# Differential attention with a feed-forward interleaved: moving when a block's inputs and the feed-forward pieces are issued

## The chip, the cores and the metric

The kernel runs on one core of a Trainium2 chip. The core has a matrix engine (TensorE, "PE" in the profile), a vector engine (VectorE, "DVE"), an engine for activation functions (ScalarE, "ACT"), a general engine (GpSimd, "POOL") and DMA queues ("SP" and others). They run side by side and wait for each other by semaphores. The metric is the time of one execution on the device in microseconds (us); lower is better.

## The reference

Four blocks are applied to `x`, of 2 batches by 1024 tokens by 256 channels, each added to its input: softmax attention, a small feed-forward, a second attention and the small feed-forward again; then differential attention, a gated feed-forward with 4-bit weights, a recurrent layer that learns while it runs, and the gated feed-forward again. What is changed lies in the differential attention and the first gated feed-forward:

```python
energy = jnp.einsum('bqhad,bkhad->bahqk', qd, kd)      # a: two halves of each head
energy = jnp.where(causal, NEG, energy)
scores = jax.nn.softmax(energy / np.sqrt(D), axis=-1)
diff = scores[:, 0] - lam * scores[:, 1]
diff = jnp.where(causal, NEG, diff)
diff = jax.nn.softmax(diff, axis=-1)
att = jnp.einsum('bhqv,bvhd->bqhd', diff, v)
att = att * rsqrt(mean(att * att) + EPS) * rms_w * (1 - LAM_INIT)
x = x + att @ Wo
x = x + (gelu(xn @ Wg.T) * (xn @ Wu.T)) @ Wd.T         # xn: layernorm of x
```

There are 16 heads with 4 key heads, of width 2 x 16 for queries and keys and 16 for values. The hidden width of the feed-forward is 2048. Everything is float32.

## The kernel before, in words

`build` runs the stages one after the other: attention, attention, feed-forward, then `attn_d_ffn1` (the differential attention and the gated feed-forward of its tiles) and `ttt_ffn1` (the recurrent layer and the last feed-forward). Only `attn_d_ffn1` is touched.

**Blocks, pairs, rounds.** Queries are cut into 8 blocks `i` of 128 tokens. A block has 8 pairs of heads in batch 0 and then 8 in batch 1, so 16 pairs; 128 pairs in all. The main loop runs over rounds `n`. Round `n` issues the scores of pair `n` (L1209), the masked row maxima (`highest`, VectorE, L1220) and the exponentials (ScalarE, L1230), and the later steps of the pairs before it: `ratio` (L1236), `difference` (L1252), `turn` (transposes on TensorE, L1267, then an exponential on ScalarE, L1274) and, for every second pair, `weigh` (L1287). Blocks 4 to 7 have more than 512 keys and are "large": their scores come in two parts. So rounds 0 to 63 are small and 64 to 127 large, and a few more rounds follow in which only later steps are left.

**Filling pieces.** Between these steps each round issues pieces of other work, kept in the dictionary `at` by round and added with `add(n, step)`. They are
- the inputs of a block (`attn_d_inputs`: layernorm statistics, normalized rows, the transpose `xT`), and then for each batch five pieces from `attn_d_block`: `queries` (a projection of 512 columns, then a rotation on VectorE and GpSimd), `keys` (the same with 192 columns, and a copy of the values by ScalarE, L1150), `turn_queries(0)`, `turn_queries(1)` (transposes, then a ScalarE copy into `qT`, L1160) and `turn_keys` (transposes, then two VectorE multiplications into `kT`, L1167);
- the output of a block (`attn_d_out`: `squares`, `root`, `normalize`, `project`);
- the feed-forward of a block's tokens (`ffn1_parts`: `stats`, `rows`, `turn`, 8 `gate` pieces, `gelu`, 8 `up` pieces, 8 `down` pieces).

A large round splits its list of filling pieces in three parts, in the order of the `add` calls; a small round splits it in two.

**Order.** `in_order` keeps TensorE, VectorE, ScalarE and GpSimd in the order in which the program issues instructions. An engine that waits holds up everything behind it.

**The one bank.** Every filling piece with a matmul takes its PSUM tile from `bank` (L1095). In small rounds two banks take turns; in large rounds there is one. A piece then can't start its matmuls before the engine that reads the piece before has emptied that bank. The accumulator of the `down` pieces holds it from the first of the eight to the last.

**Places.** Counted from the first round of block `i`, its inputs stood at -9, -8, -6; then batch 0 at -4, -4, -2, -2, -2 and batch 1 five times at -1. For block 0 all are issued ahead of round 0. The output and feed-forward of block `i` are counted from the first round of block `i+1`, a round later for blocks 0 to 2. Those of block 7 belong to the next stage, except for its output.

Of the kernel before, what the change touches and what calls it, by code (L numbers as in the profile page):

```python
# [23 lines left out]
NB = T // P  # L24
# [20 lines left out]
class Net:  # L45
# [899 lines left out]
    def attn_d_ffn1(self, w, wo, cos, sin, nlam, rms_w, deq):  # L945
# [7 lines left out]
        with ExitStack() as ctx:  # L953
# [35 lines left out]
            def add(n, *steps):  # L989
                at.setdefault(max(n, -1), []).extend(steps)  # L990

            for i in range(NB):
                n = 16 * i
                tile_ = type("tile", (), {})()
                blocks = [
                    self.attn_d_block(pools, tile_, b, i, kT[b], v[b]) for b in range(B)
                ]
                for m, step in zip(
                    (-9, -8, -6, -4, -4, -2, -2, -2, -1, -1, -1, -1, -1),
                    (*self.attn_d_inputs(ps, work, tile_, i), *blocks[0][0], *blocks[1][0]),  # L1000
                ):
                    add(n + m if i else -1, step)
                for _, units in blocks:
                    pairs.extend(units)

                n += 16
                squares, root, normalize, project = self.attn_d_out(ps, work, tile_, wo, i)
                if i == NB - 1:

                    for m, step in enumerate((squares, root, normalize, project)):  # L1010
                        add(n + 2 + m, step)
                    continue
                stats, rows, turn, gate, gelu, up, down = self.ffn1_parts(ps, work, i, deq)
                n += 1 if i < 3 else 0
                for m, step in (
                    (2, squares), (3, root), (4, normalize), (5, project), (5, stats), (6, rows),
                    (7, turn), *((8 + k // 2, gate[k]) for k in range(8)), (12, gelu),
                    *((13 + k // 2, up[k]) for k in range(8)),
                    *((17 + k // 2, down[k]) for k in range(8)),
                ):  # L1020
                    add(n + m, step)
            nothing = type("nothing", (), {"large": False})()

# [19 lines left out]
            for n in range(max(max(at), max(weighings)) + 1):  # L1043
# [8 lines left out]
                k = (len(fill) + 2) // 3, (2 * len(fill) + 2) // 3, (len(fill) + 1) // 2  # L1052
# [1042 lines left out]
```

## Time and profile before

| what | value |
|---|---|
| median of 3 runs | 3026.88 us (3020.59 to 3034.16) |
| the profiled execution's own time | 3026.56 us |
| its span, first to last instruction | 3024.8 us |
| TensorE busy | 2592.0 us, 86% of the span |
| VectorE busy | 1949.4 us, 64% |
| ScalarE busy | 1324.3 us, 44% |
| GpSimd busy | 1037.1 us, 34% |
| rounds 0 to 127 of the changed stage | about 1067.7 to 2161.8 us of the span |

A round is read off the trace by the first score matmul (L1209) of each pair. The table below names the rounds that matter later by their place in a block; the clock is the granted share of TensorE's clock, a mean.

| rounds | from, to (us) | TensorE busy | VectorE busy | clock |
|---|---|---|---|---|
| block 6, round 14 (2 `up`, 3 input pieces of batch 0) | 1950.7, 1963.6 | 10.75 | 9.20 | 1.00 |
| block 6, round 15 (2 `up`, 5 input pieces of batch 1) | 1963.6, 1989.6 | 15.06 | 12.27 | 0.82 |
| block 7, round 14 (2 `up`) | 2142.0, 2151.8 | 9.80 | 8.38 | 1.00 |
| block 7, round 15 (2 `up`) | 2151.8, 2161.8 | 8.55 | 9.67 | 1.00 |

Busy time of TensorE counts a matmul from its start to a modelled end, so it shows where the engine has something to do and not how well it does it.

### The profile page before, as it was taken

Reading aid. Unit: us, or ns where it says so; the run is one execution under the profiler, and the core shown is the slowest. Engines: PE = TensorE matmul, PEld = TensorE weight load, DVE = VectorE, ACT = ScalarE, POOL = GpSimd, SP = SyncE. Lnnn points to the kernel's source line nnn. Section 1 sums busy time; section 2 is a strip of 40 time slices with the busy share of each in tenths; the row PEclk is TensorE's granted clock in tenths of the full one; section 3 lists DMA queues with packets and bytes.
Section 4 is the critical chain, followed back from the end, with each engine's and each line's share of the span. In section 5 each row is a group of like instructions: output and inputs, shape, how many; then the busy total and the mean of one; then the engine's idle time right before and its main releaser. Section 6 shows DMA issues by size and latency. Waiting matters only on the chain.

```text
span 3024.8 us, 66879 instructions
## 1 busy us (share of the span) xinstructions
PE 2592.0 (86%) x26384; PEld 1613.2 (53%) x26384; DVE 1949.4 (64%) x6736; ACT 1324.3 (44%) x2672; POOL 1037.1 (34%) x1672
## 2 busy tenths in 40 slices
PE   6999997999988777889888778888877888888888
PEld 2334344434434444666555555555555766677777
DVE  5777665866755456757677868768646656565552
ACT  2686850454453256566565555646521212212110
POOL 3345322212115466556565646556500000000000
PEclk8999997999999856889899888988987889998999
DMA  3000000000001100000000000000001100101100
GB/s 116 1 1 1 1 1 1 1 1 1 1 15 43 28 1 1 1 1 1 1 1 1 1 1 1 1 1 1 20 15 24 24 21 19 23 14 33 24 9 15
DMA packets 61979, 35.39 MB, mean 12 GB/s; under 512 B 43216, under 2 KB 58080, under 8 KB 61664
## 3 DMA queue, kind: packets, MB, share of 16 engines
q1 hardware_dynamic: 59472, 29.49, 3.8%
q8 instruction: 208, 3.41, 0.5%
q10 hardware_dynamic: 2192, 1.61, 0.2%
q14 instruction: 107, 0.88, 0.1%
HBM read 22.68 MB, written 8.39 MB: 10 GB/s over the span
## 4 chain that ended last, share of the span: by engine, by line
PE 38%; DVE 13%; ACT 7%; issue 5%; POOL 3%; DMA 0%; POOLq 0%; ACTq 0%; DVEq 0%
PE ph L1420 6%; PE po L1929 5%; PE pg L1916 4%; PE pu L1916 4%; ACT p L1230 4%; PE e L1209 3%; DVE p L1220 3%; PE dT L1267 3%; PE po L1439 2%; DVE p L1256 2%; PE py L1287 2%; PE pq L232 1%; POOL p L1243 1%; PE pq L1599 1%; PE kh L1599 1%
## 5 line engine op out<-in xcount | busy, mean ns | idle before, releaser
L1220 DVE CUSTOM_DVE_ANT_0 p<-e,mask 128x512 f32<-128x512 f32 (+3 forms) x768 | 381.1, 552 | 67.8 <-PE e L1209 67.3
L1230 ACT ACTIVATE p<-p,nm 128x128 f32<-128x128 f32 (+7 forms) x512 | 389.7, 764 | 51.3 <-DVE nm L1220 39.6
L1274 ACT ACTIVATE pT<-dT 128x128 f32<-128x128 f32 (+7 forms) x256 | 165.6, 647 | 285.5 <-PE dT L1267 284.2
L1209 PE MATMUL e<-kT,qT 32*128 32x512 f32 (+3 forms) x1536 | 243.9, 607 | 44.9 <-DVE nm L1220 43.3
L196 POOL TENSOR_SCALAR ln_mv<-ln_mv 128x2 f32<-128x2 f32 x56 | 18.1, 324 | 728.4 <-DVE ln_mv L194 718.4
L1243 POOL TENSOR_SCALAR p<-p,ra,neg_lam 128x128 f32<-128x128 f32 (+7 forms) x256 | 215.9, 843 | 145.8 <-DVE ra L1239 120.2
L1267 PE MATMUL dT<-ident,p 128*128 128x128 f32 x1152 | 194.2, 300 | 56.0 <-ACT pT L1274 29.9
L845 ACT ACTIVATE pr<-s 128x512 f32<-128x512 f32 (+3 forms) x384 | 157.3, 496 | 162.9 <-PE s L840 154.2
L1256 DVE CUSTOM_DVE_ANT_0 p<-p,rs 128x128 f32<-128x128 f32 (+7 forms) x256 | 206.4, 832 | 32.0 <-POOL p L1247 31.9
L1267 PEld LDWEIGHTS dT<-ident,p 128*128 128x128 f32 x1152 | 147.8, 153 | 133.8 <-issue 48.2
L1260 POOL TENSOR_SCALAR p<-p,md 128x128 f32<-128x128 f32 (+7 forms) x256 | 207.0, 809 | 25.4
L550 ACT ACTIVATE pr<-s 128x1024 f32<-128x1024 f32 (+1 forms) x192 | 145.4, 813 | 131.1 <-PE s L544 82.8
L1929 PE MATMUL po<-down,inter 128*128 128x256 f32 x576 | 162.0, 444 | 6.7 <-issue 5.6
L1916 PE MATMUL pg<-xT,gate 128*128 128x256 f32 x576 | 152.8, 412 | 8.5 <-ACT xT L225 5.5
L805 PE MATMUL s<-kT,qT 32*128 32x512 f32 (+3 forms) x768 | 155.0, 518 | 4.3 <-DVE q_pad L813 2.5
L555 ACT ACTIVATE pr<-pr 128x1024 f32<-128x1024 f32 (+1 forms) x192 | 152.1, 852 | 0.0
L1420 PE MATMUL ph<-xT,up 128*128 128x256 f32 x448 | 126.2, 433 | 27.5 <-DVE inter L1428 20.5
L813 DVE CUSTOM_DVE_ANT_0 masked<-s,mask 128x128 f32<-128x128 f32 (+3 forms) x256 | 110.6, 487 | 59.2 <-PE s L805 59.0
L1209 PEld LDWEIGHTS e<-kT,qT 32*128 32x128 f32 x1536 | 91.9, 213 | 103.4 <-DVE nm L1220 74.1
L1259 POOL TENSOR_SCALAR md<-md 128x1 f32<-128x1 f32 x256 | 90.9, 355 | 161.4 <-DVE md L1256 149.6
L1929 PEld LDWEIGHTS po<-down,inter 128*128 128x128 f32 x576 | 126.8, 225 | 31.2 <-issue 7.0
L558 POOL TENSOR_SCALAR_AFFINE_SELECT pr<-pr 128x256 f32<-128x256 f32 x128 | 90.4, 724 | 153.2 <-ACT pr L555 56.2
(313 smaller groups left out, 5418.5 us busy)
## 6 DMA issues: line engine op xcount, KB each, us to landing
uk_d<-uk SPq DMA_DIRECT2D x128, 32.0 KB, 1.9
r<-uk_d SPq DMA_DIRECT2D x8, 512.0 KB, 3.9
x<-in_L_attn_a_X SPq DMA_DIRECT2D x4, 512.0 KB, 6.0
qh_d<-qh SPq DMA_DIRECT2D x8, 256.0 KB, 2.8
o<-qh_d SPq DMA_DIRECT2D x128, 16.0 KB, 1.8
out<-x SPq DMA_DIRECT2D x4, 512.0 KB, 3.1
w<-in_L_ffn_W2T SPq DMA_DIRECT2D x1, 1024.0 KB, 8.1
pk<-in_L_ffn_gate_packed SPq DMA_DIRECT2D x8, 128.0 KB, 2.5
```

The lines of the kernel that those rows point to most:

```text
L845: nc.scalar.activation(pr[:, g, off:512], tiles[g][:, 0:m], AF.Exp, scale=0.25)
L1209: nc.tensor.matmul(own.tiles[h][:, a, 0 : hi - lo], made["q"][r : r + 32, a, t, :], kT[r : r + 32, a, lo:hi], start=True, stop=True,)
L1220: nc.vector.tensor_tensor_reduce(own.p[h][a][:, lo:hi], own.tiles[h][:, a, 0 : hi - lo], neg_row[:, T - nk + lo : T - nk + hi], -1.0, 3e38 ...
L1230: nc.scalar.activation(own.p[h][a], own.p[h][a], AF.Exp, bias=own.nm[:, h, a : a + 1], scale=-1.0, accum_out=own.sm[:, h, a : a + 1],)
L1243: nc.gpsimd.tensor_scalar(p1, p1, own.ra[:, h : h + 1], nlam[:, head : head + 1], ALU.mult, ALU.mult)
L1256: nc.vector.tensor_tensor_reduce(p0, p0, p1, own.rs[:, h, 0:1], -3e38, ALU.add, ALU.max, md)
L1260: nc.gpsimd.tensor_scalar(p0, p0, md, 1.0, ALU.add, ALU.mult)
L1267: nc.tensor.transpose(dT[:, kb, :], own.p[h][0][:, kb * P : (kb + 1) * P], self.ident)
L1274: nc.scalar.activation(pT[:, 0 : qb + 1, :], dT[:, 0 : qb + 1, :], AF.Exp)
L1420: nc.tensor.matmul(ph[:, j, :], w[:, kc, m * P : (m + 1) * P], f.xT[:, kc, :], start=(kc == 0), stop=(kc == 1),)
L1916: nc.tensor.matmul(ph[:, j, :], m_[:, kc, m * P : (m + 1) * P], f.xT[:, kc, :], start=(kc == 0), stop=(kc == 1),)
L1929: nc.tensor.matmul(f.po[:, b], inter[m // 2][:, m % 2, b * P : (b + 1) * P], wd[:, m % 2, (m // 2) * C : (m // 2 + 1) * C], start=(m == 0) ...
```

## The change

It alters two lists of rounds, and adds two lines for one block; the steps and their work stay.

- Inputs: after the three common ones, batch 0's pieces stand at -5, -4, -3, -2, -1, one to a round. Batch 1's `queries` and `keys` move behind the start of the block, to 0 and 1, and its three transposing pieces to 7, the last round of batch 0's pairs. Block 0 follows the same rule: what would be ahead of round 0 is issued there, the rest in rounds 0, 1 and 7.
- Output and feed-forward: from `project` and `stats` on, everything is a round later. `squares`, `root`, `normalize` stay.
- For block 6 (`NB - 2`) the first added line takes that round back, and the second moves the later pieces forward: its `up` pieces then fall into rounds 125, 126 (four of them) and 127, and its `down` pieces into 128 (four), 129 and 130. Before, they were two to a round from 125 to 132.

```diff
                 for m, step in zip(
-                    (-9, -8, -6, -4, -4, -2, -2, -2, -1, -1, -1, -1, -1),
+                    (-9, -8, -6, -5, -4, -3, -2, -1, 0, 1, 7, 7, 7),
                     (*self.attn_d_inputs(ps, work, tile_, i), *blocks[0][0], *blocks[1][0]),
                 ):
-                    add(n + m if i else -1, step)
+                    add(n + m, step)
...
                 for m, step in (
-                    (2, squares), (3, root), (4, normalize), (5, project), (5, stats), (6, rows),
-                    (7, turn), *((8 + k // 2, gate[k]) for k in range(8)), (12, gelu),
-                    *((13 + k // 2, up[k]) for k in range(8)),
-                    *((17 + k // 2, down[k]) for k in range(8)),
+                    (2, squares), (3, root), (4, normalize), (6, project), (6, stats), (7, rows),
+                    (8, turn), *((9 + k // 2, gate[k]) for k in range(8)), (13, gelu),
+                    *((14 + k // 2, up[k]) for k in range(8)),
+                    *((18 + k // 2, down[k]) for k in range(8)),
                 ):
+
+                    m -= 1 if i == NB - 2 and m > 4 else 0
+                    m -= (m - 12) // 3 if i == NB - 2 and m > 12 else 0
                     add(n + m, step)
```

## The prediction

> **What bounds the kernel now.** I read the page first, then busy time by stretch, then TensorE's waits, then the instructions in order of time. By the page TensorE is the busiest engine and carries most of the chain that ended last.
>
> ```profile
> span 3024.8 us, 66879 instructions
> ...
> PE 2592.0 (86%) x26384; PEld 1613.2 (53%) x26384; DVE 1949.4 (64%) x6736; ACT 1324.3 (44%) x2672; POOL 1037.1 (34%) x1672
> ...
> PE 38%; DVE 13%; ACT 7%; issue 5%; POOL 3%; DMA 0%; POOLq 0%; ACTq 0%; DVEq 0%
> ```
>
> An average over the whole kernel says little about one stage, so I cut the changed stage at the first score matmul of each pair. First blocks 6 and 7 whole, then some rounds. The columns are the stretch, its length, the busy time of TensorE, its weight loads, VectorE, ScalarE and GpSimd, and the mean granted clock.
>
> ```profile
> 1800.60:1989.60 189.00, 153.15 (x1153) 101.13 (x1153) 139.97 (x439) 108.54 (x179) 108.00 (x143) 0.89 0.00 1
> 1989.60:2161.80 172.20, 148.80 (x1215) 97.91 (x1214) 141.42 (x409) 109.95 (x164) 107.59 (x128) 0.91 0.00 1
> ```
>
> Block 6 works on 7 key tiles and block 7 on 8, yet block 6 takes 16.8 us longer. What only block 6 has is the loading of the next block's inputs. The next rows show where: rounds 14 and 15 of block 6, the round behind them, and rounds 14 and 15 of block 7, which have the same `up` pieces and no inputs.
>
> ```profile
> 1950.70:1963.60 12.90, 10.75 (x117) 7.70 (x116) 9.20 (x27) 7.37 (x13) 5.96 (x8) 1.00 0.01 2
> 1963.60:1989.60 26.00, 15.06 (x65) 8.70 (x65) 12.27 (x37) 11.99 (x22) 12.14 (x16) 0.82 0.00 0
> 1989.60:2000.80 11.20, 11.20 (x103) 7.77 (x102) 6.61 (x21) 0.92 (x1) 2.76 (x4) 0.81 0.01 1
> 2142.00:2151.80 9.80, 9.80 (x117) 7.22 (x116) 8.38 (x25) 6.57 (x10) 6.52 (x8) 1.00 0.00 0
> 2151.80:2161.80 10.00, 8.55 (x55) 5.55 (x54) 9.67 (x28) 6.77 (x11) 6.53 (x8) 1.00 0.01 2
> ```
>
> 38.9 us stand against 19.8, and in round 15 no engine is busy for more than 15.06 of 26.00 us. TensorE's waits in those two rounds of block 6 (total, times, longest) say why:
>
> ```profile
> PE t_ps L1165 <- ACT qT L1160: 5.1, 1, 5.1
> PE ph L1420 <- DVE inter L1428: 3.4, 2, 1.9
> PE t_ps L1159 <- ACT v L1150: 2.3, 1, 2.3
> PE ph L1420 <- DVE kT L1167: 0.8, 1, 0.8
> PE pq L232 <- DVE inter L1428: 0.8, 1, 0.8
> PE t_ps L1159 <- ACT qT L1160: 0.7, 1, 0.7
> ```
>
> Each is a filling piece waiting for the one bank. The longest in order of time:
>
> ```profile
> 1983.30 0.63 PE L1159 MATMUL t_ps<-ident,qr 128*128 128x128 f32 x4
> ...
> 1988.29 0.58 ACT L1160 ACTIVATE qT<-t_ps 128x512 f32<-128x512 f32 x1
> 1988.98 0.29 PEld L1165 LDWEIGHTS t_ps<-ident,kr 128*128 128x128 f32 x2 [5.30 <-issue]
> 1989.01 0.66 PE L1165 MATMUL t_ps<-ident,kr 128*128 128x128 f32 x2 [5.09 <-ACT qT L1160]
> ```
>
> The transposes end at 1983.9; the copy that frees the bank takes 0.58 us but stands in ScalarE behind one `turn` and four exponentials, and TensorE, its next piece wanting that bank, sits still.
>
> **What the Trainium skill says.** "Perfetto Trace Analysis", Per-engine timelines: ScalarE, VectorE and GpSimd are strict FIFO, and TensorE only pulls weight loads ahead. The 5.09 us above agree. "PSUM — Partial Sum Buffer", PSUM bank collisions: two engines must not touch a bank's quadrant at once, so accesses are ordered by semaphores, by bank; the six waits agree. "TensorE: Matmul & The Clock Gate", Part 1: after an idle window of about 3.4 us TensorE's clock is halved until it has been busy for a window. Here the clock is 0.82 in the round with the long waits and 0.81 in the next, and 1.00 in the three others.
>
> **The change part by part.** The pieces' own work is the same before and after, wherever it stands; TensorE does it in either place. So I count waits, not work. No moved piece issues a DMA, so SP and GpSimd's queues carry none of it; the GpSimd additions of the rotation move with their piece.
>
> (a) *Rounds 14 and 15 ahead of blocks 5, 6, 7.* The same answer for the other two boundaries lists 10.0 and 11.1 us; with 13.1 above, 34.2 us. One input piece per round beside two `up` pieces leaves little: block 7 with its two `up` per round waits 0.8 us on them in rounds 126 to 130. As a check, 38.9 minus 19.8 minus the eight pieces' own time is 12.9, near 13.1. The own time (6.2, estimate): 6.68 us busy at clock 0.69 for batch 1 ahead of round 0, so 4.6 at full clock, and 1.6 for the other three. I take -34.
>
> (b) *Clock.* At 0.82 and 0.81, 15.06 and 11.20 busy us lose 2.7 and 2.1. The other two boundaries have 0.99 and 0.84, then 0.90 and 0.75, for 11.21, 9.30, 13.07 and 11.10 busy us: 1.6 and 4.1. Of these 10.5 I take about half back: -6.
>
> (c) *Boundaries of blocks 1 to 4.* Small rounds have two banks. Their waits, without those behind `gelu` (which only moves), are 3.8, 3.2, 3.4 and 4.3: -15. In block 0 rounds are about 3 us, TensorE busy for two; its rounds 11 to 15 take 31.7 us, half of it input pieces. Spread, they partly fill that idle time: -4 more.
>
> (d) *Ahead of round 0.* Batch 1's five pieces run from 1058.7 to 1067.7, 9.0 us with nothing beside them. They come back in rounds 0, 1 and 7 with about 6 us, as the clock is half there: -3.
>
> (e) *`project` two rounds behind `normalize`.* Its wait for yT is 5.8 us in all, of which 2.4 is block 6's, whose places don't move: -3.4.
>
> (f) *New waits at the head of the keys.* `turn_keys` of batch 0 is now the last piece before the scores that read it, and batch 1's the last before round 8: 14 places. TensorE stops until VectorE has multiplied into `kT`; behind it stand that round's scores, and behind these VectorE's maxima and all exponentials. The trace has the same piece at the same place, one round earlier, where nothing waits for it: from the end of the transposes to the end of `kT` it takes 0.65 us at five boundaries, then 1.06, then 1.86. From zero (VectorE would have been late anyway) to 2 us; I take 1.1: +15.
>
> (g) *The moved pieces' bank waits in their new rounds.* `queries` in round 0 leaves the bank to a rotation (0.8 us waited for the like today), `keys` to a ScalarE copy (2.0 in the worst rounds: ph behind v, 6.0 in three), round 7 to two `qT` copies. Per large block 2.5, four of them: +10; nothing to 20.
>
> (h) *The end.* Four `up` in round 126 bring 3.8 us forward plus 0.8 of waits; four `down` instead of two `up` in 128 add 3.8, of which about 2 fall into the 4.6 us that TensorE waits there now. So the last weighing comes 6.5 us later. Behind it, before, 17.8 us pass until the output projection (2181.3 to 2199.1), since 24 `down` matmuls are left and VectorE stands behind a load that lands at 2187.5. With 8 left, the chain of VectorE work that follows the load (to 2192.4, then 1.5 us) ends it: some 13.2. +2. The next stage's loads start at the last weighing and move with it.
>
> Sum: -34 -6 -19 -3 -3 +15 +10 +2 = -38. From the profiled execution's 3026.6 that is 2988; it stands 0.3 below the median of 3026.9, so this holds for both. What is late next: VectorE's maxima (the scores wait for nm 43.3 us over the stage) and `gelu`, which both stay.
>
> **The rivals.**
> *The spread rounds cost nothing* (0.13): (f) and (g) vanish since VectorE and ScalarE keep pace, and the clock recovers all of (b). -38 -25 -5 gives about 2959. For it: rounds with two `up` or `down` and no inputs have TensorE busy throughout. Against: VectorE is busy 74% of block 6.
> *The waits move* (0.11): the one bank is the cause, not the crowd, and each piece waits wherever it is. Twice to three times (g), and (a) only half: within 15 us of 3026. For it: `keys` alone in round 12 delays the next piece by 2 us. Against: blocks 6 and 7 above.
> *Slower, by the keys' place* (0.06): (f) with a whole VectorE backlog. Without (f) the change is worth 53 us; at 14 places it breaks even at 3.8 us each and is slower by 0.5% from 4.9. At 5 us: 3027 - 53 + 70 = 3044. For it: the lag grows with the block. Against: its largest today is 1.86.
> That nothing changes is excluded: the compiled order of TensorE has `queries` behind block 6's last `up` pieces, in the next block's round 0. Feed-forward pieces were two to a round before, too; that half moves a wait or two, (e).
>
> **How the numbers follow.** My case has 0.70, its own range 2962 to 3010 from the ends of (f), (g) and (b). 0.5% is about what a measurement of this kernel tells from no change: 15 us, so 3012 is the edge. Faster: 0.70 + 0.13, less a little; same: 0.11 and that little; slower 0.06. The range, 2950 to 3012, takes in the first rival and leaves out the other two.
>
> **What would show it.** (a): no round at a boundary above some 16 us, and t_ps behind qT nearly gone from the list of waits. (b): clock above 0.9 there. (d): the first scores some 9 us earlier. (e): yT gone but for block 6. (f): a new entry, scores behind kT, of about 15 us; over 50 makes me wrong. (g): `ph` behind rope or v. (h): the last weighing later than the rounds' gain tells, a shorter way behind it. The recurrent stage must stay as long as it is; if it doesn't, the cause is none of these.

## The result and the profile after

| | before | after |
|---|---|---|
| median of 22 runs each | 3023.35 us (3016.48 to 3035.82) | 3016.42 us (3006.32 to 3021.55) |
| profiled execution, its span | 3026.56 us, 3024.8 us | 3017.59 us, 3015.8 us |

The ratio is 0.9966, with 0.9955 to 0.9976 as its 95% interval: faster by 0.34%, some 10 us. The forecast was 2988 us, 38 us less, with 3012 us as the upper end of its range.

The page of the kernel after, its first lines and its chain, has nothing to see but a shorter span:

```profile
span 3015.8 us, 66875 instructions
...
PE 2597.2 (86%) x26384; PEld 1621.9 (54%) x26384; DVE 1953.4 (65%) x6736; ACT 1323.2 (44%) x2672; POOL 1026.8 (34%) x1672
...
PE 38%; DVE 13%; ACT 7%; issue 5%; POOL 2%; DMA 0%; ACTq 0%; POOLq 0%; DVEq 0%
```

The same cut by stretches as in the prediction: block 6, then its rounds 13, 14 and 15, round 0 of block 7, and rounds 14 and 15 of block 7. The columns are again the stretch, its length, busy TensorE, weight loads, VectorE, ScalarE, GpSimd, and the clock.

```profile
1794.80:1975.70 180.90, 150.84 (x1153) 101.69 (x1152) 137.36 (x440) 107.93 (x180) 104.31 (x143) 0.89 0.00 1
1935.99:1945.61 9.62, 5.93 (x35) 3.52 (x34) 5.29 (x20) 7.64 (x14) 6.57 (x10) 0.82 0.01 3
1945.61:1961.47 15.86, 12.58 (x107) 8.68 (x107) 10.08 (x31) 11.14 (x13) 5.94 (x8) 0.89 0.01 2
1961.47:1975.74 14.27, 10.34 (x49) 7.17 (x48) 8.16 (x26) 6.20 (x12) 5.94 (x8) 0.76 0.00 0
1975.74:1987.66 11.92, 11.18 (x108) 7.30 (x107) 10.80 (x30) 8.00 (x14) 6.75 (x9) 1.00 0.01 2
2131.38:2147.45 16.07, 13.91 (x130) 10.14 (x129) 10.93 (x29) 9.04 (x14) 7.19 (x9) 0.98 0.00 1
2147.45:2157.45 10.00, 9.18 (x92) 6.53 (x94) 9.30 (x27) 6.19 (x11) 6.12 (x9) 1.00 0.00 0
```

Block 6 is 8.1 us shorter. Its round 15 went from 26.0 to 14.3 us, as the prediction wanted; but its round 14 went from 12.9 to 15.9, and the two together still have 7.2 idle us of TensorE in 30.1, at a clock of 0.89 and 0.76.

All the parts of the stage in one table (us, from one trace each; cut at the first score matmul of each pair, the last weighing, and the first transpose of the stage's and of the next stage's layernorm). The other kernels are those of the experiments.

| kernel | before round 0 | block 0 | blocks 1-3 | blocks 4-6 | block 7 to last weighing | on to next stage | stage |
|---|---|---|---|---|---|---|---|
| before | 20.3 | 63.8 | 337.1 | 520.9 | 191.7 | 25.9 | 1159.8 |
| after | 11.6 | 62.2 | 343.9 | 509.0 | 200.6 | 22.2 | 1149.6 |
| e1, inputs alone | 11.6 | 62.5 | 332.3 | 524.1 | 198.3 | 24.2 | 1153.0 |
| e2, feed-forward alone | 20.4 | 63.5 | 341.4 | 533.5 | 199.7 | 23.0 | 1181.4 |
| e3, no block 6 line | 11.6 | 62.2 | 343.9 | 509.0 | 196.1 | 27.1 | 1150.0 |
| e5, `tq0` off `gelu` | 11.6 | 62.2 | 340.5 | 503.1 | 200.1 | 22.3 | 1139.9 |
| e6, small blocks old | 11.6 | 70.2 | 336.9 | 501.2 | 200.6 | 22.4 | 1142.9 |
| e11, small feed-forward old | 10.9 | 62.4 | 336.0 | 503.1 | 201.7 | 22.4 | 1136.4 |
| e8, before without `gelu` | 20.4 | 63.5 | 321.7 | 508.7 | 186.7 | 28.0 | 1129.1 |
| e9, after without `gelu` | 11.6 | 62.2 | 318.6 | 487.8 | 194.4 | 22.3 | 1096.9 |
| e10, before, copies on VectorE | 20.3 | 60.0 | 331.3 | 516.4 | 188.6 | 27.3 | 1144.0 |
| e7, after, copies on VectorE | 11.7 | 61.4 | 338.6 | 484.9 | 198.5 | 22.5 | 1117.5 |
| e12, combined | 11.7 | 61.1 | 333.7 | 470.3 | 195.6 | 25.6 | 1098.0 |

The way to round 0 gives 8.7 us and blocks 4 to 6 give 11.9. Blocks 1 to 3, which should have gained, lose 6.8. TensorE's waits over blocks 4 to 6 (total, times, longest) show what became of the gain there. Of the names, e are the scores, dT the transposes of `turn`, py the weighing, t_ps the transposing pieces, ph the `gate` and `up` pieces, po the output and `down` pieces. Before:

```profile
PE e L1209 <- DVE nm L1220: 23.1, 19, 2.3
PE ph L1420 <- DVE inter L1428: 16.8, 10, 2.9
PE t_ps L1165 <- ACT qT L1160: 13.2, 3, 5.1
PE ph L1420 <- ACT xT L225: 10.1, 3, 4.0
PE dT L1267 <- POOL p L1260: 7.0, 9, 1.8
PE ph L1420 <- ACT v L1150: 6.0, 3, 2.3
PE t_ps L1159 <- ACT v L1150: 5.6, 3, 2.3
```

After (from `attn_d_ffn1` on the lines are four further down):

```profile
PE dT L1271 <- POOL p L1264: 15.1, 6, 3.1
PE e L1213 <- DVE nm L1224: 11.5, 13, 2.8
PE py L1291 <- ACT pT L1278: 10.8, 3, 4.3
PE ph L1424 <- ACT xT L225: 10.1, 3, 4.0
PE ph L1424 <- ACT qT L1164: 9.8, 3, 3.7
PE t_ps L1163 <- ACT v L1154: 8.4, 3, 3.5
...
PE po L1443 <- ACT v L1154: 2.6, 2, 1.4
PE t_ps L1169 <- ACT qT L1164: 2.1, 3, 0.7
...
PE ph L1424 <- DVE rope L268: 1.3, 3, 0.5
PE ph L1424 <- ACT v L1154: 1.3, 1, 1.3
...
PE ph L1424 <- DVE inter L1432: 0.4, 1, 0.4
```

The predicted waits did go: t_ps behind qT (13.2 to 2.1), ph behind inter (16.8 to 0.4), ph behind v (6.0 to 1.3). Others came in their place: py behind pT and ph behind qT from nothing to 10.8 and 9.8, dT behind p from 7.0 to 15.1 (while e behind nm fell from 23.1 to 11.5), t_ps behind v from 5.6 to 8.4. All entries of the list together fall only from 98.8 to 83.2 us.

The two that are new, py behind pT and ph behind qT, stand in the very rounds that were to be freed. In rounds 14 and 15 of blocks 4, 5 and 6 TensorE waited 10.0, 11.1 and 13.1 us before, and it waits 7.3, 6.9 and 7.4 us after: of 34.2 us 21.6 are left, and all but 1.0 of these are py behind pT and ph behind qT. The same list for these two rounds of block 6 alone (1945.6 to 1975.7 us) begins with

```profile
PE ph L1424 <- ACT qT L1164: 3.7, 1, 3.7
PE py L1291 <- ACT pT L1278: 3.1, 1, 3.1
```

Both in order of time, from rounds 13 to 15 of block 6:

```profile
1943.92 1.28 ACT L1435 ACT_TABLE_LOAD   x1
1945.22 3.62 ACT L1435 ACTIVATE inter<-inter 128x4096 f32<-128x4096 f32 x1
1948.85 1.28 ACT L1278 ACT_TABLE_LOAD   x1
1950.15 0.92 ACT L1278 ACTIVATE pT<-dT 128x896 f32<-128x896 f32 x1
...
1951.12 3.20 PE L1291 MATMUL py<-pT,v 128*32 128x128 f32 x50 [3.06 <-ACT pT L1278]
...
1960.88 0.66 PE L1163 MATMUL t_ps<-ident,qr 128*128 128x128 f32 x4 [0.21 <-DVE inter L1432]
...
1965.69 0.57 ACT L1164 ACTIVATE qT<-t_ps 128x512 f32<-128x512 f32 x1
...
1966.32 3.78 PE L1424 MATMUL ph<-xT,up 128*128 128x256 f32 x8 [3.71 <-ACT qT L1164]
```

First the weighing waits for a `turn` exponential that stands in ScalarE behind `gelu` and two table loads (`ACT_TABLE_LOAD`, one ahead of `gelu` and one behind it), 6.2 us together. Then the transposes of `turn_queries(1)`, round 14's input piece, are done by 1961.6, but the 0.57 us copy that frees the one bank stands behind four exponentials, and the next `up` piece waits 3.71 us. That is the prediction's picture of round 15 (a copy late in ScalarE) in a new round, with another piece behind it.

In small rounds the same engine is late for `turn`. Block 2, rounds 14 and 15:

```profile
1322.58 1.28 ACT L1435 ACT_TABLE_LOAD   x1
1323.87 3.62 ACT L1435 ACTIVATE inter<-inter 128x4096 f32<-128x4096 f32 x1
1327.51 1.28 ACT L1234 ACT_TABLE_LOAD   x1
...
1331.21 0.57 ACT L1164 ACTIVATE qT<-t_ps 128x512 f32<-128x512 f32 x1
1331.69 0.47 ACT L1278 ACTIVATE pT<-dT 128x384 f32<-128x384 f32 x1
...
1332.30 0.87 PE L1271 MATMUL dT<-ident,p 128*128 128x128 f32 x3 [7.78 <-ACT pT L1278]
```

TensorE stands still for 7.78 us: the `turn` exponential that it needs stands behind `gelu`, its two table loads, four exponentials and a copy. The longest such wait before was 5.4 us. Over the stage this wait grew from 29.9 us (27 times) to the first of these lines; the second is new, and the third, the wait (f) of the prediction, was 0.8 us, once, before:

```profile
PE dT L1271 <- ACT pT L1278: 42.2, 34, 7.8
...
PE pkv L232 <- ACT inter L1430: 6.5, 3, 2.6
...
PE e L1213 <- DVE kT L1171: 3.5, 8, 0.6
```

### The profile page after: what moved, and what is told of

It is laid out like the page before. It is cut to its first block, busy times and chain, and to the rows that moved or that the text cites. A ratio compares the mean times of both kernels' runs of the same rounds, so it can differ in the third digit from the quotient of the medians.

```text
span 3015.8 us, 66875 instructions
## 1 busy us (share of the span) xinstructions
PE 2597.2 (86%) x26384; PEld 1621.9 (54%) x26384; DVE 1953.4 (65%) x6736; ACT 1323.2 (44%) x2672; POOL 1026.8 (34%) x1672
## 4 chain that ended last, share of the span: by engine, by line
PE 38%; DVE 13%; ACT 7%; issue 5%; POOL 2%; DMA 0%; ACTq 0%; POOLq 0%; DVEq 0%
PE ph L1424 6%; PE pg L1920 5%; PE po L1933 5%; ACT p L1234 4%; PE pu L1920 4%; DVE p L1224 3%; PE dT L1271 3%; PE e L1213 3%; PE po L1443 2%; DVE p L1260 2%; PE py L1291 2%; PE pq L232 1%; PE pq L1603 1%; PE pa L1603 1%; PE kh L1603 1%
## 5 line engine op out<-in xcount | busy, mean ns | idle before, releaser
L196 POOL TENSOR_SCALAR ln_mv<-ln_mv 128x2 f32<-128x2 f32 x56 | 14.2, 254 | 724.2 <-DVE ln_mv L194 714.0
L1271 PE MATMUL dT<-ident,p 128*128 128x128 f32 x1152 | 196.9, 303 | 65.5 <-ACT pT L1278 42.2
L1260 DVE CUSTOM_DVE_ANT_0 p<-p,rs 128x128 f32<-128x128 f32 (+7 forms) x256 | 214.5, 864 | 40.4 <-POOL p L1251 40.4
L1264 POOL TENSOR_SCALAR p<-p,md 128x128 f32<-128x128 f32 (+7 forms) x256 | 203.7, 796 | 25.4
L558 POOL TENSOR_SCALAR_AFFINE_SELECT pr<-pr 128x256 f32<-128x256 f32 x128 | 90.7, 726 | 154.9 <-ACT pr L555 62.5
L1920 PE MATMUL pu<-xT,up 128*128 128x256 f32 x576 | 141.2, 389 | 0.2 <-issue 0.2
L1926 DVE TENSOR_TENSOR inter<-inter,pu 128x512 f32<-128x512 f32 x72 | 49.4, 686 | 140.9 <-PE pu L1920 138.1
```

What stands on the lines that cost most here:

```text
L1260: nc.vector.tensor_tensor_reduce(p0, p0, p1, own.rs[:, h, 0:1], -3e38, ALU.add, ALU.max, md)
L1264: nc.gpsimd.tensor_scalar(p0, p0, md, 1.0, ALU.add, ALU.mult)
L1271: nc.tensor.transpose(dT[:, kb, :], own.p[h][0][:, kb * P : (kb + 1) * P], self.ident)
L1920: nc.tensor.matmul(ph[:, j, :], m_[:, kc, m * P : (m + 1) * P], f.xT[:, kc, :], start=(kc == 0), stop=(kc == 1),)
```

## The experiments

Ratios are to before, with their 95% intervals. e1, e2, e8 and e10 are shown as edits of the kernel before, the others as edits of the kernel after. The recurrent stage behind, untouched, varied by 11 us from one trace to another (last section), so single traces are compared by the columns of the table and not by their spans.

### e1 and e2: each half alone

e1 keeps the feed-forward as before and takes the new rounds of the inputs; batch 1's `keys` go to round 0, because in round 1 the old `down` pieces still hold the bank. That the feed-forward is a round later is what gives `keys` its place.

```diff
-                    (-9, -8, -6, -4, -4, -2, -2, -2, -1, -1, -1, -1, -1),
+                    (-9, -8, -6, -5, -4, -3, -2, -1, 0, 0, 7, 7, 7),
...
-                    add(n + m if i else -1, step)
+                    add(n + m, step)
```

> The inputs' new rounds with the feed-forward's old ones; batch 1's keys go to round 0 beside its queries, since in round 1 the down pieces hold the bank. First theory, the waits move: a spread piece waits for ScalarE in its new round too, because the gelu and the exponentials stand ahead of its copy; blocks 4 to 6 gain about 10 us, blocks 1 to 3 nothing, block 0 some 8: 10 to 18 us faster than before in all. Rival, the spread is worth what was forecast and the feed-forward's shift loses it again: 25 us faster or more.

e2 takes the feed-forward's new rounds, with block 6's two lines, and leaves the inputs as they were.

```diff
-                    (2, squares), (3, root), (4, normalize), (5, project), (5, stats), (6, rows),
+                    (2, squares), (3, root), (4, normalize), (6, project), (6, stats), (7, rows),
...
+                    m -= 1 if i == NB - 2 and m > 4 else 0
+                    m -= (m - 12) // 3 if i == NB - 2 and m > 12 else 0
```

> The feed-forward's new rounds with the inputs' old ones. The waits move: the shift alone is worth little either way, within 8 us of before (the wait for yT gone, 3 us; block 6's four up pieces in one round, 2 us lost). Rival, the shift is what eats the spread's gain: 15 us slower or more, most of it in blocks 1 to 6.

Measured: e1 3009.31 us, 0.9951 [0.9929, 0.9972]; e2 3040.02 us, 1.0048 [1.0031, 1.0064]. By these the inputs alone give at least what the whole change gives; by the stage in the traces they give 6.8 us where the whole change gives 10.2 (1159.8 to 1153.0 and to 1149.6), so which of the two is the faster is not told. The feed-forward alone costs 0.5%. By the table e1 gains at the start and in blocks 1 to 3 (337.1 to 332.3), and nothing in blocks 4 to 6, where most was expected (520.9 to 524.1). e2 loses 12.6 us there. Its waits over the whole stage are led by the very one that the prediction called the cost of the boundary, 15.0 us in five waits before and 5.1 at the longest:

```profile
PE t_ps L1168 <- ACT qT L1163: 41.0, 9, 8.9
```

Of these, 27.8 us are in blocks 0 to 3, where `gelu` now falls into round 14 beside the old places of batch 0's transposing pieces. In blocks 4 to 6 this wait is 13.2 us, as before; what grew there is dT behind p (7.0 to 24.1) and py behind pT, the weighing behind `gelu` (nothing to 8.5). By the stage, e1's -6.8 and e2's +21.6 do not add up to the change's -10.2. So the halves are not two additive terms: what shares a round with `gelu` and the exponentials matters.

### e3: without the bunching in block 6

```diff
-                    m -= (m - 12) // 3 if i == NB - 2 and m > 12 else 0
```

> The changed kernel without the line that moves block 6's up and down pieces forward; they stay two to a round. From the traces the four up pieces in round 126 cost 6.3 us, and 4.4 of it come back until the next stage starts, so this should be about 2 us faster than the changed kernel, 12 than before. Rival, that line is what spoils block 7 (8.8 us longer up to the last weighing than before): 5 us or more faster than the changed kernel.

Measured: 3013.56 us, 0.9958 [0.9942, 0.9975], not to be told from after (0.9966). In the trace the last weighing comes 4.5 us earlier (200.6 to 196.1) and the way behind it is 4.9 us longer (22.2 to 27.1). The line moves time from one side of the last weighing to the other; the prediction's (h) had the two nearly cancel as well.

### e5, e6, e11: other rounds for a few pieces

e5 moves the first transposing piece of batch 0, so that none shares the round of `gelu`:

```diff
-                    (-9, -8, -6, -5, -4, -3, -2, -1, 0, 1, 7, 7, 7),
+                    (-9, -8, -6, -5, -4, -2, -2, -1, 0, 1, 7, 7, 7),
```

> The changed kernel, with batch 0's first turn_queries moved from round 13, where the large blocks now have the gelu, to round 14 beside the second. If the place beside the gelu costs, the wait of the next up piece for qT (9.8 us in three large rounds) goes, and blocks 4 to 6 get 6 to 9 us shorter. Rival, the copy waits for the exponentials anyway: blocks 4 to 6 the same within 2 us, and the wait shows up in round 14 under another name.

Measured: 3004.60 us, 0.9926 [0.9913, 0.9938], better than after. Over blocks 4 to 6 (509.0 to 503.1) t_ps behind v is gone (8.4 in after), while this line of e5 says that the wait behind the qT copy stayed as long as it was (9.8):

```profile
PE ph L1423 <- ACT qT L1163: 10.0, 3, 3.9
```

On that wait the rival is right: the copy waits for the exponentials with or without `gelu` in the round. But the copy waited for is that of the second piece, `turn_queries(1)`, which stands last in round 14 in both kernels. In block 6 of e5 the two copies of that round come at

```profile
1946.06 0.60 ACT L1163 ACTIVATE qT<-t_ps 128x512 f32<-128x512 f32 x1 [0.53 <-PE t_ps L1162]
...
1951.90 0.58 ACT L1163 ACTIVATE qT<-t_ps 128x512 f32<-128x512 f32 x1
```

The first starts 0.03 us after its transposes end, the second 4.5 us after, behind four exponentials, since a large round issues the last third of its pieces behind them. So it is the place within the round, and not the round alone, that makes the copy late. A move within the round was not tried.

e6 gives the small blocks back both halves:

```diff
                 for m, step in zip(
+                    (-9, -8, -6, -4, -4, -2, -2, -2, -1, -1, -1, -1, -1) if 0 < i < 5 else
                     (-9, -8, -6, -5, -4, -3, -2, -1, 0, 1, 7, 7, 7),
...
-                    m -= 1 if i == NB - 2 and m > 4 else 0
+                    m -= 1 if (i < 3 or i == NB - 2) and m > 4 else 0
```

> The changed kernel with the old lists in the small rounds: inputs of blocks 1 to 4 and feed-forward of blocks 0 to 2 as before, block 0's start and all large blocks as changed. If the small rounds lose by the change itself, as the traces say (blocks 1 to 3 took 6.7 us longer), this is 6 to 8 us faster than the changed kernel, 16 to 18 than before. Rival, the 6.7 us are what block 0 had gained and gave back through late engines: no more than 2 us from the changed kernel.

Measured: 3001.05 us, 0.9912 [0.9889, 0.9935]. By the stage in the traces the size is as expected, 6.7 us less than after and 16.9 less than before; by the medians it is 25 us less than before, more than expected. The place is not as expected: blocks 0 to 3 in sum are no shorter (406.1 to 407.1), since block 0 now carries block 1's inputs at its end, beside its own pieces in rounds 0, 1 and 7 (62.2 to 70.2), while blocks 1 to 3 gain 7.0. What is shorter is block 4, by 7.8 us in the trace: its batch 1 is finished in round 63, where two banks take turns, and no longer in rounds 64, 65 and 71, where there is one. That reading comes from the trace alone and was not isolated.

e11 gives back only the feed-forward of blocks 0 to 2, with the new inputs:

```diff
-                    m -= 1 if i == NB - 2 and m > 4 else 0
+                    m -= 1 if (i < 3 or i == NB - 2) and m > 4 else 0
```

> The changed kernel with the feed-forward of blocks 0 to 2 at its old places, inputs as changed. If the shift of the gelu to round 14 beside the spread inputs is what lost time in the small rounds, blocks 1 to 3 get 8 to 12 us shorter, to about 332 us, and the kernel 8 to 12 us faster than the changed one. Rival, it is batch 1's pieces in rounds 0, 1 and 7 that cost there: blocks 1 to 3 shorten by less than 4.

Measured: 3002.25 us, 0.9917 [0.9900, 0.9934], faster than after by 14 us. Blocks 1 to 3 fall from 343.9 to 336.0, below before's 337.1, and dT behind pT from 42.2 to 35.9 us. The loss of blocks 1 to 3 is the feed-forward's later round, not the inputs, which gain them 1.1 us. Another 5.9 us went in blocks 4 to 6 (509.0 to 503.1), where nothing was edited.

### e8 and e9: before and after without `gelu`

In both, the `gelu` of this stage does nothing, so in 14 of the 16 feed-forward tiles (not 8, as the first expectation says) the hidden values go on without the activation and the output differs. The pieces around it stay where they were.

```diff
         def gelu():
-            nc.scalar.activation(f.inter, f.inter, AF.Gelu_apprx_tanh)
+            pass
```

> The kernel before with the gelu of this stage left out (8 of the 16 feed-forward tiles are then multiplied without it; the last tile's and the last stage's stay). Each gelu holds ScalarE for 3.6 us and two loads of tables of 1.3 us, seven times: 43 us of ScalarE, of which 20 to 40 us should show. It is the base for the next run.

> The changed kernel with the same gelu left out. If the gelu in ScalarE's queue is what eats the spread's gain, the change is worth 25 us or more without it: this is at least 25 us faster than the kernel before without gelu. Rival, the one bank and the exponentials do it with or without gelu: 5 to 15 us faster than that kernel, as with gelu.

Measured: e8 2990.44 us, 0.9892 [0.9873, 0.9911]; e9 2965.02 us, 0.9792 [0.9773, 0.9811]. Seven times 6.18 us are 43 us of ScalarE's time, and it is only 44% busy; leaving them out gives 36 us on before (3026.91 beside it) and 51 on after. Without `gelu` the change is worth 25.4 us (2965.02 / 2990.44 = 0.9915) in place of 10, and by the stage 32.2 (1129.1 to 1096.9). By the table `gelu` costs blocks 1 to 3 15.4 us before and 25.3 after, and blocks 4 to 6 12.2 before and 21.2 after: in the changed order it costs 9.9 and 9.0 us more. Of the two waits left in rounds 14 and 15 of blocks 4 to 6, py behind pT (10.8) is gone in e9 and ph behind qT stays (9.6). dT behind pT, 42.2 us after, is in e9

```profile
PE dT L1270 <- ACT pT L1277: 18.5, 31, 1.4
```

### e7 and e10: the bank's copies on VectorE

If the wait is a matter of ScalarE's queue, another reader of the bank must free it sooner. In e7 (on after) and e10 (on before) the qT and v copies go to VectorE:

```diff
-            nc.scalar.copy(
+            nc.vector.tensor_copy(
                 v[:, qb, :, 0:D], pkv[:, 128:192].rearrange("p (g d) -> p g d", d=D)
...
-            nc.scalar.activation(made["q"][:, a], pt, AF.Copy, scale=0.25)
+            nc.vector.tensor_scalar_mul(made["q"][:, a], pt, 0.25)
```

> The changed kernel with the copies that empty the bank after turn_queries and keys (qT, v) on VectorE and no longer on ScalarE. If ScalarE's queue is what holds the bank, TensorE's waits for qT and v (24 us in all after the change) go and the kernel is 10 to 20 us faster than the changed one. Rival, any reader's queue does it: VectorE gets 22 us more work, the waits for it grow by as much, within 5 us of the changed kernel.

> The kernel before, with the copies of qT and v on VectorE as in the run on the changed kernel that gained 37 us. Theory, the spread is worth what was forecast as soon as ScalarE's queue no longer holds the bank: in the old crowd five pieces still follow each other through one bank, so this gains less, 10 to 23 us, and the change on top of it is worth 25 or more. Rival, the copies are worth the same with either order: 30 to 40 us faster than before, and the change is worth 10 here too.

Measured: e7 2978.93 us, 0.9850 [0.9834, 0.9866]; e10 3004.60 us, 0.9928 [0.9912, 0.9944]. e7 gains 37.5 us on after, where 10 to 20 were expected; e10 gains 20, within its 10 to 23. VectorE is busier than ScalarE (65% against 44%) and still the better place. With these copies the change is worth 0.9850 / 0.9928 = 0.9921, and in blocks 4 to 6 31.5 us (516.4 to 484.9), a little more than the 28 that the prediction had for them. Blocks 1 to 3 lose as much as without (331.3 to 338.6): so the copies leave that loss as it was. e7's waits in blocks 4 to 6:

```profile
PE py L1290 <- ACT pT L1277: 10.2, 3, 3.9
...
PE t_ps L1162 <- DVE qT L1163: 7.4, 3, 2.9
...
PE ph L1423 <- DVE qT L1163: 2.3, 3, 1.0
...
PE t_ps L1162 <- DVE v L1153: 0.5, 1, 0.5
```

ph behind qT goes from 9.8 to 2.3 and t_ps behind v from 8.4 to 0.5; the wait behind `gelu`, py behind pT, stays. VectorE has a queue too: 7.4 us of t_ps behind qT are new, all in round 7, where batch 1's three transposing pieces stand together. The copies also leave ScalarE less to do before its exponentials, and blocks 4 to 6 gained 24.1 us (509.0 to 484.9), more than these waits. What the bank's sooner release is worth and what the lighter ScalarE was not separated.

### e12: what the experiments point to

On after: e11's line for the small blocks and e7's copies, the copies of the inputs' `xT` on VectorE too (10.1 us of ph behind xT in the lists of before and after), and without block 6's bunching line. e7's part of the edit is left out here:

```diff
-                    m -= 1 if i == NB - 2 and m > 4 else 0
-                    m -= (m - 12) // 3 if i == NB - 2 and m > 12 else 0
+                    m -= 1 if (i < 3 or i == NB - 2) and m > 4 else 0
...
-            tile_.xT = self.layernorm_turn(work, pt, tile_.xn, False)
+            tile_.xT = self.layernorm_turn(work, pt, tile_.xn, False, True)
```

> What the runs point to, together: the changed kernel, with the copies of qT, v and the inputs' xT on VectorE, the feed-forward of blocks 0 to 2 at its old places, and without the line that bunches block 6's up pieces. If the gains add: 37 for qT and v, 8 for the small rounds, 2 for block 6 and up to 8 for xT (12.4 us of waits behind it) on the changed kernel's 10: 55 to 65 us faster than before. Rival, VectorE is full by now and xT only trades one queue for another: 45 to 50.

Measured: 2956.86 us (2953.65 to 2961.64), 0.9772 [0.9753, 0.9790], faster than before by 2.3%, which is 68 us where 55 to 65 were expected, and than after by 60 us. e7 and e11 alone give 37.5 and 14.2 us against after, 51.7 together; if these add, the other 8 come from `xT` and block 6's line, which were not separated.

The stretch from the first scores to the last weighing in before, after, e7 and e12, one view each:

```profile
1067.70:2181.20 1113.50, 916.18 (x6653) 616.56 (x6652) 795.26 (x2866) 652.48 (x1415) 669.78 (x1129) 0.86 0.00 1
```

```profile
1060.50:2176.20 1115.70, 929.81 (x6702) 632.32 (x6702) 801.01 (x2875) 653.05 (x1417) 662.41 (x1133) 0.86 0.00 1
```

```profile
1058.50:2141.90 1083.40, 907.40 (x6703) 614.30 (x6704) 819.63 (x2920) 634.21 (x1371) 664.33 (x1134) 0.88 0.00 1
```

```profile
1058.40:2119.10 1060.70, 896.77 (x6671) 608.95 (x6671) 823.59 (x2925) 631.52 (x1365) 669.61 (x1133) 0.88 0.00 1
```

## Why the prediction was wrong

Its sign was right, its size was not: about -10 us in place of -38. By its steps:

- **(a), the waits ahead of blocks 5, 6, 7, -34.** This is the step that failed: "One input piece per round beside two `up` pieces leaves little." Its signs came: t_ps behind qT is nearly gone, block 6's round 15 fell from 26.0 to 14.3 us, and no such round is above 16.2. But rounds 14 and 15 still hold 21.6 of the 34.2 us, so the step brought -12.6. The evidence for it was block 7, whose rounds have the `up` pieces and no input piece. Two waits took the old ones' place. 9.8 us are `up` pieces waiting for a bank whose qT copy stands in ScalarE behind four exponentials: e5 has this wait with no transposing piece in `gelu`'s round (10.0), e9 without any `gelu` (9.6), and e7, with VectorE as the reader, has 2.3. The other 10.8 us are weighings behind `gelu`, which moved with the feed-forward and was priced at nothing; in e9 they are gone. Blocks 4 to 6 as a whole, for which the prediction's terms ((a), most of (b) and (e), three of the four blocks of (g), six of the 14 places of (f)) gave about -28, came to -11.9. The change is worth -31.5 there with the copies on VectorE in both kernels, and -20.9 without `gelu` in both.
- **(g), +10, nothing to 20, for the moved pieces' waits in their new rounds.** For what it priced, batch 1's pieces in rounds 0, 1 and 7, it was right: in blocks 4 to 6 they make po behind v 2.6, ph behind rope 1.3, ph behind v 1.3 and t_ps behind qT 2.1, together 7.3 us, where it had 7.5. For batch 0's pieces, which now wait and make others wait in rounds 13 to 15, it had nothing: ph behind qT is one of these waits, and t_ps behind v (8.4, where ph behind v was 6.0) the other.
- **(c), -15 for the small boundaries.** Wrong in sign for blocks 1 to 3: +6.8, where three of its four boundaries gave -10.9. It left out the waits behind `gelu`, "which only moves". It does move, by one round, and in the changed order it costs more: 9.9 us in blocks 1 to 3 and 9.0 in blocks 4 to 6 (e8 and e9 by the table), and e11, with the whole feed-forward of the small blocks back, regains 7.9 in blocks 1 to 3. With the feed-forward at its old place the direction of (c) holds: e1 gains 4.8 us in blocks 1 to 3, less than half of its size. For the way in and block 0, (d) with -3, the -4 of (c) and its first boundary, -3.8, come to -10.8; the trace has -10.3.
- **(b), the clock, -6.** Nothing came. The prediction's working, with busy time and clock of the same three rounds at each of the three boundaries, gives 11.7 us lost after, for 10.5 before. The loss moved: the round behind the boundary is at 1.00 now (0.75 to 0.84 before), but rounds 14 and 15 are at 0.76 to 0.89, where above 0.9 was to show it right.
- **(e), yT, -3.4.** Right, and a little more: the entry, 5.8 us before, is gone altogether.
- **(f), scores behind kT, +15.** Mis-sized: 3.5 us in 8 waits, 0.6 at the longest. Its own list had 0.8 us of ph behind kT at the place where it says that nothing waits. That VectorE's maxima are late anyway, so that the scores seldom find kT last, is a reading and was not tested.
- **(h), the end, +2.** The sum holds, its parts less so. From round 126 to the last weighing the traces have 39.36 us before and 44.95 after, so 5.6 later (6.5 was said), and the way behind it is 3.7 shorter (4.6 was said): +1.9. Two misses of 0.9 cancel.

Of the rivals, "the waits move" came nearest, with a time within 15 us of 3026 and (a) only half done; little more than a third of it was done. Its cause, the one bank, is behind 9.8 of the 21.6 us left in rounds 14 and 15; the 10.8 behind `gelu` are not the bank's, and no rival named them. That "each piece waits wherever it is" does not hold either: e5 has one qT copy at once and one late in the same round. In the small blocks the cause is the later feed-forward (e11), and by e9 its `gelu`. The slow case by the keys' place is excluded by (f)'s 3.5 us.

What stays open: why block 4 gains in e6 and e11 when the edit is in smaller blocks (one bank or two is the reading for e6, not isolated), why dT behind p and e behind nm change places in the large blocks, and what the change is worth with `gelu` out and the copies on VectorE at once, which no run has.

## What to carry to other kernels

Before moving a piece that shares one PSUM bank, look at the queue of the engine that empties it: the reader's place behind the long instructions of its round sets how long the bank is held (0.03 and 4.5 us for two like copies in one round of e5), and a new round is only better if that place is. Price a wait that vanishes only as high as the next wait behind it allows, and when several pieces move by "only a round", list for the long ones (here `gelu`, 6.2 us with its table loads) what will stand behind them. The better cure here was not a new round but another reader for the bank, although that engine was the busier one: 20 us on the kernel before (e10), where the change gave 10.

## What the runs showed of the hardware that was not expected

- Waits that went took more time with them than their length. From after to e7 the stretch from first scores to last weighing has the same matmuls (6702 and 6703) and is 32.3 us shorter; only 9.9 of these are idle time of TensorE (185.9 to 176.0), the other 22.4 are shorter matmuls (busy 929.81 to 907.40), beside a granted clock of 0.88 for 0.86. That agrees with the Trainium skill's "TensorE: Matmul & The Clock Gate", Part 1, on what idle windows do to the clock; the prediction had counted the clock in the boundary rounds alone, and half of it. A part may be of the execution and not of the edit: the recurrent stage, which is alike in both, was 5.7 us (0.7%) shorter in e7's trace, which on 930 us of matmuls would be some 6.5 of the 22.4 us (an estimate).
- The recurrent stage, with the same instructions in the same order in every kernel here, took between 807 and 818 us from one trace to the next (817.6 before, 817.3 after, 807.3 in e1), while the changed stage's blocks in after and e3, where their code is alike, agree within 0.1 us. Where so small a gain is traced, the stage and not the span has to be compared.
- Each `gelu` among the exponentials costs two table loads of 1.28 us beside its 3.62 us (4096 elements a partition), so two fifths of `gelu`'s hold on ScalarE (2.56 of 6.18 us) aren't the function. The Trainium skill's "ScalarE activation tables: per-element evaluation and per-set limits", What a function is on this engine, has 1283 ns for one load, and the trace agrees; the prediction had not counted it, since it left `gelu` out.
